# Cross attention: the first two tiles' scores placed among the last heads of the query phase

## The chip, the core and the metric

The kernel runs on one core of a Trainium2 chip. The metric is the device time of one execution in microseconds (us). Before the change it is 1665.28 us, the median of 3 runs (1662.88 to 1666.53). Abbreviations: PE is TensorE (PEld its weight loads), DVE is VectorE, ACT is ScalarE, POOL is GpSimd, SP is SyncE. SBUF is the working memory, PSUM the memory of 8 banks that PE writes to.

## What is computed

The reference is a decoder of four layers on `x` (8 sequences of 56 tokens, 256 channels). Each layer has self attention, cross attention to a context (8 sequences of 1500 positions, 64 channels) and a feed-forward part, each followed by a residual sum and a layer norm. The change touches three of the four cross attentions, those of layers 0, 2 and 3, which are built alike (16 heads of 128 channels, keys compressed to 64 channels; rotary queries in layers 0 and 2). For one sequence they compute

```
q      = x @ Wq                      # per head, 128 channels
qa     = rope(q @ w_kc_q) @ (W_qr @ W_kr.T)   # per head, 64 channels: the query against the compressed keys
e      = exp(scores - row maximum)   # scores = qa @ kv.T, 1500 positions
heads  = (e @ kv) / sum(e)
x      = layernorm(x + heads @ (w_kc_kv, Wo folded into one matrix wm))
```

Layer 3 has no rope, so its matrices are folded into one per head before `x` is touched.

## The kernel before

`decoder_kernel` runs twelve steps in order; a step's weights are loaded during the step before it by SP's DMA queue. The cross attention is `xattn` (line 686). It has two phases.

**Query phase** (pools `xq`, PSUM as two buffers of two banks and three of one bank, line 698). `x_weights` or `x_weights3` builds the small matrices, `turn_x` transposes X, and `x_context` starts the loads of the first two sequences' keys (`kvT`, on POOL's queue). Then `x_queries` (line 799, stages 1 and 2, which are layers 0 and 2) goes over the heads with a software pipeline: in round h it projects head h+3 (PE, one bank `ps_qh`; ACT copies it to `qh`), makes head h+2's rope (PE `ps_big`, two DVE multiplications, two POOL additions), and in odd rounds computes `qa` for the pair h-1, h with `pair_of` (line 744): 8 matmuls into one bank `ps_qk`, two ACT copies (line 754). Each half of `qa`'s 128 partitions holds one head of the pair; after every second pair two DMAs on ACT's queue (line 759) bring the columns of the last two pairs to the other half of the partitions. In rounds 3, 7 and 11 `rows_of` issues four DMAs on ACT's queue for a third of the first sequence's key rows (`kv`). `x_queries3` (line 761, stage 3, which is layer 3) has only `pair_of`, with `rows_of` ahead of heads 4, 8 and 12.

**Tile loop** (`x_tiles`, line 864; pools `xs` and `psx`, which take the memory of the query phase's, all 8 PSUM banks as one tile `ps_x`). A sequence has 16 x 56 = 896 queries, that is 7 tiles of 128; 8 sequences make 56 tiles. A tile n has two halves u; each covers 375 keys from the beginning and 375 from the middle of the 1500.

- `scored(n, u)` (891): the scores of a half, one matmul per half of the partitions (4 instructions in the trace), into two banks. There are four score banks, so two halves can be in flight.
- `moved(n, u)` (902): one DVE instruction copies the half to SBUF (`sc`, three buffers) and keeps its extremum in `tops`.
- `weights(n)` (917): ACT's exponential over the 1500 scores, with the sum.
- `turned(n)` (925): DVE's 32 x 32 block transpose into `cells` (the tile `eT`).
- `gather(b, j)` (932): PE's product of the transposed weights of sequence b with its `kv`, worked on during the tiles of sequence b+1.
- `weighted` and `kept` (947, 958): four portions of `wm`, made by PE and copied by ACT in rounds 0, 1, 13 and 20.

What sets the order: `ordered` (372, called `do` or, for matmuls, `pe` here) ties each instruction to the one that the program laid out before it on the same engine. All of `x_tiles` and `pair_of`'s matmuls are laid out so, and the query phase's other matmuls are held in program order too; ACT's copies, the ropes on DVE and POOL are not tied, the framework places them. Each engine then works its list in order. In the loop, round n lays out scores of half 1 of tile n+2 and half 0 of tile n+3, `moved(n+2, 0)`, what there is of `gather` and `weighted`, `turned(n)`, `moved(n+2, 1)` and `weights(n+1)`.

Of the kernel before, what the change touches and what calls it, by code (L numbers as in the profile page):

```python
# [9 lines left out]
F32 = mybir.dt.float32  # L10
# [15 lines left out]
KL = KB * NKB  # L26
# [238 lines left out]
class Decoder:  # L265
# [420 lines left out]
    def xattn(self, n):  # L686
        nc, tc = self.nc, self.tc
        qrT, krT = self.rowsets(f"l{n}x_r", 192), self.rowsets(f"l{n}x_k", DC)
        kckv, wo = self.rowsets(f"l{n}x_v", DC), self.rowsets(f"l{n}x_o", D)

        with tc.tile_pool(name="xa", bufs=1) as outer:


            wm = outer.tile([128, 8, D], F32, name="wm")


            qa = outer.tile([128, NB * NQ], F32, name="qa")
            with tc.tile_pool(name="xq", bufs=2) as pool, self.psum(2, 3):
                rotary = n != 3
                wqk = (self.x_weights if rotary else self.x_weights3)(pool, qrT, krT)  # L700
                self.turn_x(range(NT))
                context = self.x_context(outer)
                (self.x_queries if rotary else self.x_queries3)(n, pool, wqk, qa, context[2])
            with tc.tile_pool(name="xs", bufs=1) as pool, tc.tile_pool(name="psx", bufs=1, space=PSUM) as banks:
                self.x_tiles(pool, banks.tile([128, 8, 512], F32, name="ps_x"), qa, wm, kckv, wo, *context)

    def x_weights(self, pool, qrT, krT):

# [49 lines left out]
                rows, others = (slice(u * DC, (u + 1) * DC) for u in (odd, 1 - odd))  # L758
                nc.scalar.dma_start(flat[others, :, odd, cols], flat[rows, :, odd, cols])

    def x_queries3(self, n, pool, wqk, qa, rows_of):


        xT = self.xT
        kcq = [a.rearrange("p (j k) -> p j k", j=8) for a in self.parts(f"l{n}x_c")]
        wq = [a.rearrange("p (j k m) -> p j k m", j=2, k=2) for a in self.parts(f"l{n}x_q")]
        halves = [slice(odd * DC, (odd + 1) * DC) for odd in range(2)]

        m2 = pool.tile([128, 2, 8, DC], F32, bufs=1, name="m2")
        for four in range(2):  # L770
            ps = self.bank2("ps_m2")[:, :, : 4 * DC].rearrange("p u (j d) -> p u j d", d=DC)
            for j in range(4 * four, 4 * four + 4):
                for part in range(3):
                    for odd, rows in enumerate(halves):
                        self.ordered(
                            self.nc.tensor.matmul, ps[:, odd, j % 4], kcq[part][rows, j, :], wqk[rows, part, j],
                            start=part == 0, stop=part == 2,
                        )
            for k in range(2):
                self.by_parity(lambda rows, odd: (m2[rows, k, 4 * four : 4 * four + 4], ps[halves[k], odd]))  # L780
        m3 = pool.tile([128, 2, 8, 2, DC], F32, bufs=1, name="m3")
        for four in range(2):
            ps = self.bank2("ps_m3").rearrange("p u (j c d) -> p u j c d", c=2, d=DC)
            for j in range(4 * four, 4 * four + 4):
                for c in range(2):
                    for k in range(2):
                        for odd, rows in enumerate(halves):
                            self.ordered(
                                self.nc.tensor.matmul, ps[:, odd, j % 4, c],
                                wq[j // 2][rows, j % 2, k, c * 128 : (c + 1) * 128], m2[rows, k, j],  # L790
                                start=k == 0, stop=k == 1,
                            )
            self.by_parity(lambda rows, odd: (m3[:, odd, 4 * four : 4 * four + 4], ps[:, odd]))
        for h in range(0, 16, 2):
            if h and h % 4 == 0:
                rows_of(0, h // 4 - 1)
            self.pair_of(self.bank("ps_qk"), qa, h, [[(m3[:, odd, h // 2, c], xT[:, c, :]) for c in range(2)] for odd in range(2)])

    def x_queries(self, n, pool, wqk, qa, rows_of):
        xT, nc = self.xT, self.nc  # L800
        wq, kcq = self.heads(f"l{n}x_q"), self.rowsets(f"l{n}x_c", 192)

        def table(name):
            return self.const(name).rearrange("p (a s) -> p a s", a=2).unsqueeze(2).to_broadcast([96, 2, NB, S])

        cos, sin = table("xq_cos"), table("xq_sin")

        heads, ropes = {}, {}

        def projected(h):  # L810
            ps = self.bank("ps_qh")
            self.mm(ps[:, :T], [(wq(c, h), xT[:, c, :]) for c in range(2)], fixed=True)
            qh = heads[h] = pool.tile([128, T], F32, name="qh")
            nc.scalar.copy(qh, ps[:, :T])

        def rotated(h):
            qh = heads.pop(h)
            big = self.bank2("ps_big")
            for half in range(2):
                self.mm(big[:96, half, :T], [(kcq(h)[:, half * 96 : (half + 1) * 96], qh)], fixed=True)  # L820
            view = big[:96, :, :T].rearrange("p a (b s) -> p a b s", b=NB)
            rope = ropes[h] = pool.tile([96, 2, T], F32, bufs=5, name="rope")
            turn = pool.tile([96, 2, T], F32, name="turn")
            nc.vector.tensor_tensor(rope.rearrange("p a (b s) -> p a b s", b=NB), view, cos, ALU.mult)  # L824
            nc.vector.tensor_tensor(turn.rearrange("p a (b s) -> p a b s", b=NB), view, sin, ALU.mult)  # L825
            for half in range(2):
                nc.gpsimd.tensor_tensor(rope[:, half, :], rope[:, half, :], turn[:, 1 - half, :], ALU.add)  # L827


        for h in range(-3, 16):  # L830
            if h + 3 < 16:
                projected(h + 3)
            if 0 <= h + 2 < 16:
                rotated(h + 2)
            if h >= 0 and h % 2:
                if h % 4 == 3 and h < 12:
                    rows_of(0, h // 4)
                self.pair_of(
                    self.bank("ps_qk"), qa, h - 1,
                    [[(wqk(half, g), ropes[g][:, half, :]) for half in range(2)] for g in (h - 1, h)],  # L840
                )

    def x_context(self, pool):

        nc, kvs, kvTs = self.nc, {}, {}
# [15 lines left out]
        columns(1)  # L861
        return kvs, kvTs, rows_of, columns

    def x_tiles(self, pool, P, qa, wm, kckv, wo, kvs, kvTs, rows_of, columns):

# [8 lines left out]
        nc = self.nc  # L876
# [1 line left out]
        NI, NJ, CELL, do = 7, 6, 8 * KB, self.ordered  # L878
        mv = self.moments()
        sums, es, diags = {}, {}, {}  # L880
        sc4, acc = P[:, 0:4], P[:, 4:8]
        cells = pool.tile([128, NI * NI * CELL], F32, name="eT").rearrange("p (r c n) -> p r c n", r=NI, c=NI)
        scs = [pool.tile([128, KL], F32, name=f"sc{j}") for j in range(3)]
        for sc in scs:
            do(nc.gpsimd.memset, sc[:, L:], 0.0)
        num, other, rec = (pool.tile([128, 512], F32, name=name) for name in ("num", "other", "rec"))

        def pe(*args, **kw):
            do(nc.tensor.matmul, *args, **kw)

        def scored(n, u):
            b, i = divmod(n, NI)
            at = b * NQ + i * 128
            for half in range(2):
                rows = slice(half * DC, (half + 1) * DC)
                first = half * (HL - KB * (NKB - KP)) + u * QL
                pe(
                    sc4[:, 2 * u + half, :QL], qa[rows, at : at + 128], kvTs[b][rows, first : first + QL],
                    start=True, stop=True,
                )  # L900

        def moved(n, u):

            b, i = divmod(n, NI)
            if u == 0:
                if i == 0:
                    sums[b] = pool.tile([128, 8], F32, bufs=3, name="sums")
                es[n] = scs[n % 3], pool.tile([128, 4], F32, bufs=4, name="tops")
            sc, tops = es[n]
            halves = sc[:, :L].rearrange("p (u n) -> p u n", u=2)  # L910

            do(
                nc.vector.tensor_scalar, halves[:, :, u * QL : (u + 1) * QL], sc4[:, 2 * u : 2 * u + 2, :QL], 1.0,
                tops[:, 0:1] if u else None, ALU.mult, ALU.min, accum_out=tops[:, u : u + 1],
            )

        def weights(n):
# [3 lines left out]
                nc.scalar.activation,  # L921
                e[:, :L], e[:, :L], AF.Exp, bias=tops[:, 1:2], scale=-1.0, accum_out=sums[b][:, i : i + 1],
            )

        def turned(n):
            b, i = divmod(n, NI)
# [110 lines left out]
            do(nc.vector.bn_aggr, mv[:, t, :], st)  # L1037

        end, wms = NB * NI, (0, 1, 13, 20)
        for n in range(2):  # L1040
            for u in range(2):
                scored(n, u)
                moved(n, u)
        weights(0)
        scored(2, 0)
        for n in range(end):
            b, i = divmod(n, NI)
# [16 lines left out]
                    output(t, 1)  # L1064
            elif n in wms:
                weighted(wms.index(n))
            turned(n)
            if n + 2 < end:
                moved(n + 2, 1)
            if n + 1 < end:  # L1070
                weights(n + 1)
            if n in wms:
                kept(wms.index(n))
# [825 lines left out]
```

## Time and profile before

| | |
|---|---|
| median of 3 runs | 1665.28 us |
| the profiled execution's own time | 1665.35 us |
| its span | 1663.1 us (37875 instructions) |
| busy share of the span | PE 90%, DVE 66%, ACT 38%, POOL 19% |
| mean granted clock of PE | 0.926 |
| score matmuls `ps_x<-kvT,qa` | x1344, 310.4 us busy |
| block transposes `eT<-sc` | x168, 297.1 us busy, mean 1768 ns |
| reduces `sc<-ps_x`, first and second half | x168 each, means 936 and 959 ns |
| exponentials `sc<-sc,tops` | x168, mean 1544 ns |

The 168 are 56 tiles in three stages. The stages by the trace, from the first score matmul to the end of the tile loop and its tail: 219.3 to 451, 851.4 to 1085 and 1355.9 to 1590 us. A row of busy times counts an instruction from start to end, so neighbours on DVE that overlap a little show more than their spacing. A wait is named by what ended last before it; where that had long been done, it was something else. The granted clock is the share of PE's full clock that its throttle let through.

### The profile page before, as it was taken

The page shows a single profiled execution, that of the slowest core. Times are in us where ns is not written, and L with a number is a line of the kernel's source. Part 1 is how long each engine was busy: PE and PEld are TensorE (multiplying, and loading weights), DVE is VectorE, ACT ScalarE, POOL GpSimd, SP SyncE. Part 2 cuts the span into 40 slices and gives each one's busy share as a digit, 9 for nine tenths or more (in the row PEclk, how much of TensorE's full clock was granted, in tenths as well). Part 3 has the DMA queues.
Part 4 walks back from the last instruction along what each step waited for, and adds up shares of the span by engine and source line. Part 5 has one row for each costly group of instructions (what it writes and reads, how often), then busy time and mean ns, then how long its engine had stood idle before and what let it go on. Part 6 is the DMA issues. An engine that isn't in the chain of part 4 may idle for free.

```text
span 1663.1 us, 37875 instructions
## 1 busy us (share of the span) xinstructions
PE 1499.5 (90%) x16428; PEld 894.4 (54%) x16428; DVE 1095.2 (66%) x1793; ACT 625.2 (38%) x915; POOL 323.9 (19%) x302
## 2 busy tenths in 40 slices
PE   7989989999788678998989999899987978999898
PEld 4666435556644344565435555655555834555656
DVE  0575579999475855326569999635474239999633
ACT  2431245655312422103245556332343144566320
POOL 4711511212123010011521122101131000221200
PEclk9999979999897878999988999999997987999989
DMA  9523422323020001222332322121220361323100
GB/s 359 188 79 108 123 56 84 96 83 88 18 87 28 26 27 35 78 70 74 114 86 62 110 78 81 41 64 55 83 64 27 119 172 38 104 72 88 41 1 11
DMA packets 52088, 133.76 MB, mean 80 GB/s; under 512 B 20673, under 2 KB 21137, under 8 KB 51922
## 3 DMA queue, kind: packets, MB, share of 16 engines
q1 hardware_dynamic: 19906, 65.36, 12.0%
q10 hardware_dynamic: 28368, 50.25, 10.8%
q0 software_dynamic: 3648, 15.73, 2.9%
q8 instruction: 129, 2.11, 0.5%
q14 instruction: 37, 0.30, 0.1%
HBM read 119.06 MB, written 6.75 MB: 76 GB/s over the span
## 4 chain that ended last, share of the span: by engine, by line
PE 49%; DVE 9%; issue 8%; ACT 2%; DMA 1%; POOL 1%; ACTq 1%; DVEq 0%; POOLq 0%
PE ps_x L376 17%; PE ps_glu L368 8%; PE ps_y L368 7%; PE ps_qk L1675 2%; DVE sc L376 2%; PE ps_v L1675 2%; PE ps_qh L368 2%; PE ps_big L368 1%; PE ps_y L1675 1%; PE ps_q L368 1%; PE ps_qk L376 1%; PE ps_m L376 1%; PE ps_s L1397 1%; DVE E L1418 1%; DVE mx L1415 1%
## 5 line engine op out<-in xcount | busy, mean ns | idle before, releaser
L376 PE MATMUL ps_x<-kvT,qa 64*128 64x375 f32 x1344 | 310.4, 567 | 29.1 <-DVE sc L376 23.1
L376 ACT ACTIVATE sc<-sc,tops 128x1500 f32<-128x1500 f32 x168 | 259.2, 1544 | 151.7 <-DVE sc L376 118.3
L376 DVE STREAM_TRANSPOSE eT<-sc 128x1536 f32<-128x1536 f32 x168 | 297.1, 1768 | 11.7 <-PE ps_x L376 9.5
L376 PE MATMUL ps_x<-eT,kv 32*64 32x224 f32 x9024 | 257.7, 357 | 3.7 <-issue 3.2
L376 PEld LDWEIGHTS ps_x<-eT,kv 32*64 32x64 f32 x9024 | 197.6, 133 | 70.1 <-issue 59.8
L376 PEld LDWEIGHTS ps_x<-kvT,qa 64*128 64x128 f32 x1344 | 114.3, 201 | 187.2 <-DVE sc L376 160.4
L376 DVE TENSOR_SCALAR_CACHE_REDUCE sc<-ps_x 128x750 f32<-128x750 f32 x168 | 157.3, 936 | 38.4 <-PE ps_x L376 38.2
L376 DVE TENSOR_SCALAR_CACHE_REDUCE sc<-ps_x,tops 128x750 f32<-128x750 f32 x168 | 161.1, 959 | 1.3 <-PE ps_x L376 1.1
L376 POOL TENSOR_TENSOR eT<-eyes,sums 128x224 f32<-128x224 f32 x24 | 13.3, 555 | 453.6 <-DVE sums L376 453.6
L827 POOL TENSOR_TENSOR rope<-rope,turn 96x448 f32<-96x448 f32 x64 | 71.0, 1130 | 65.0 <-DVE turn L825 65.0
L824 DVE TENSOR_TENSOR rope<-ps_big,consts 96x896 f32<-96x896 f32 x32 | 34.8, 1086 | 58.4 <-PE ps_big L368 58.4
L1190 ACT ACTIVATE act<-ps_glu 128x448 f32<-128x448 f32 (+1 forms) x52 | 28.3, 544 | 111.7 <-PE ps_glu L368 108.4
L1194 DVE TENSOR_TENSOR act<-ps_glu,act 128x448 f32<-128x448 f32 x43 | 26.8, 624 | 65.2 <-ACT act L1190 65.1
L418 ACT ACTIVATE rstd<-rstd 112x3 f32<-112x3 f32 (+2 forms) x21 | 4.3, 204 | 166.2 <-DVE rstd L417 166.1
L624 DVE RECIPROCAL rec<-rec 128x896 f32<-128x896 f32 x8 | 46.0, 5753 | 27.0 <-ACT rec L623 27.0
L376 PE MATMUL ps_x<-wm,qa 128*112 128x128 f32 (+1 forms) x336 | 53.5, 318 | 9.7 <-DVE qa L376 9.7
L450 DVE TENSOR_TENSOR X<-X,ps_y 112x256 f32<-112x256 f32 x32 | 13.5, 421 | 70.6 <-PE ps_y L368 70.6
L376 PEld LDWEIGHTS ps_x<-wm,qa 128*112 128x112 f32 x336 | 45.2, 191 | 21.7 <-issue 11.2
L1758 POOL TENSOR_TENSOR qk<-qk,sw 128x896 f32<-128x896 f32 x16 | 33.3, 2083 | 101.3 <-DVE sw L1757 78.8
L376 POOL TENSOR_TENSOR qa<-num,rec 64x448 f32<-64x448 f32 x42 | 47.9, 1140 | 2.9
L754 ACT COPY qa<-ps_qk 64x448 f32<-64x448 f32 x48 | 25.3, 527 | 60.0 <-PE ps_qk L376 46.1
L376 POOL DMA_DIRECT2D kvT<-kvT x24 | 13.7, 573 | 122.7 <-DVE X L450 49.2
(410 smaller groups left out, 2424.2 us busy)
## 6 DMA issues: line engine op xcount, KB each, us to landing
kv<-kv ACTq DMA_DIRECT2D x288, 128.0 KB, 2.7
kvT<-kvT POOLq DMA_DIRECT2D x24, 384.0 KB, 3.5
qa<-qa ACTq DMA_DIRECT2D x24, 224.0 KB, 3.6
raw<-in_ctx ACTq DMA_DIRECT2D x6, 512.0 KB, 4.3
kv<-raw POOLq DMA_DIRECT2D x6, 512.0 KB, 4.2
kvT<-by POOLq DMA_DIRECT2D x6, 512.0 KB, 4.3
l0a_q<-in_l0a_q SPq DMA_DIRECT2D x4, 512.0 KB, 10.6
l0a_c<-in_l0a_c SPq DMA_DIRECT2D x4, 512.0 KB, 8.8
```

What stands on the lines that cost most here:

```text
L368: ins = self.nc.tensor.matmul(out, lhsT, rhs, start=n == 0, stop=n == len(terms) - 1)
L376: call(*args, **kw)
L624: nc.vector.reciprocal(rec, rec)
L754: nc.scalar.copy(flat[rows, :, odd, h // 2 * S : (h // 2 + 1) * S], ps[rows, :T].rearrange("p (b s) -> p b s", b=NB))
L824: nc.vector.tensor_tensor(rope.rearrange("p a (b s) -> p a b s", b=NB), view, cos, ALU.mult)
L827: nc.gpsimd.tensor_tensor(rope[:, half, :], rope[:, half, :], turn[:, 1 - half, :], ALU.add)
L1190: nc.scalar.activation(act, ps[:m, 0, :T], AF.Silu)
L1194: nc.vector.tensor_tensor(act, ps[:m, 1, :T], act, ALU.mult)
L1397: tc.keep_in_program_order(nc.tensor.matmul(*args, **kw))
L1415: nc.vector.tensor_reduce(mx, view, AX.X, ALU.max)
L1675: tc.keep_in_program_order(nc.tensor.matmul(*args, **kw))
L1758: nc.gpsimd.tensor_tensor(qk, qk, sw, ALU.add)
```

## The change

The generator `x_tiles` is now started before the query phase ends. `scored`, `moved` and `weights` of tiles 0 and 1 are laid out in four portions inside the query phase: in `x_queries` after rounds 9, 10, 13 and 14 (each portion a half of a tile, with the exponential behind the second half), in `x_queries3` after heads 8 and 10 (one portion each) and 14 (two). For this a two-bank PSUM tile of its own, `ps_x`, holds one half at a time; it comes out of the query phase's PSUM, which keeps two one-bank buffers in place of three. `sc`, `sums` and `tops` move to the pool that lasts through both phases. Once the tile loop's memory is there, the loop begins with the transposes of tiles 0 and 1 together and the scores of tile 2. Rounds 0 and 1 then have no transpose of their own, and their exponentials are those of tiles 2 and 3; round 2 has none.

```diff
-            with tc.tile_pool(name="xq", bufs=2) as pool, self.psum(2, 3):
+            with tc.tile_pool(name="xq", bufs=2) as pool, self.psum(2, 2):
...
+                tiles = self.x_tiles(outer, qa, wm, kckv, wo, *context)
+                tiles.send(None)
+                tiles.send(self.psa.tile([128, 2, 512], F32, name="ps_x"))
+                (self.x_queries if rotary else self.x_queries3)(n, pool, wqk, qa, context[2], tiles)
...
+                try:
+                    tiles.send((pool, banks.tile([128, 8, 512], F32, name="ps_x")))
+                except StopIteration:
+                    pass
...
+            for _ in range({8: 1, 10: 1, 14: 2}.get(h, 0)):
+                next(tiles)
...
+            if h in (9, 10, 13, 14):
+                next(tiles)
...
+        first = yield
+        sc_of = lambda u: first
+        scs = [outer.tile([128, KL], F32, name=f"sc{j}") for j in range(3)]
...
+        for n in range(2):
+            for u in range(2):
+                yield
+                scored(n, u)
+                moved(n, u)
+            weights(n)
+        pool, P = yield
+        sc4, acc = P[:, 0:4], P[:, 4:8]
+        sc_of = lambda u: sc4[:, 2 * u : 2 * u + 2]
...
-        for n in range(2):
-            for u in range(2):
-                scored(n, u)
-                moved(n, u)
-        weights(0)
+        turned(0)
+        turned(1)
         scored(2, 0)
...
-            turned(n)
+            if n > 1:
+                turned(n)
             if n + 2 < end:
                 moved(n + 2, 1)
-            if n + 1 < end:
+
+            if n < 2:
+                weights(n + 2)
+            elif 2 < n + 1 < end and n != 2:
                 weights(n + 1)
```

More of the change, by code (lines that the diff above doesn't have):

```diff
@@ L702, in xattn @@
                 context = self.x_context(outer)
-                (self.x_queries if rotary else self.x_queries3)(n, pool, wqk, qa, context[2])
+                tiles = self.x_tiles(outer, qa, wm, kckv, wo, *context)
+                tiles.send(None)
+                tiles.send(self.psa.tile([128, 2, 512], F32, name="ps_x"))
+                (self.x_queries if rotary else self.x_queries3)(n, pool, wqk, qa, context[2], tiles)
             with tc.tile_pool(name="xs", bufs=1) as pool, tc.tile_pool(name="psx", bufs=1, space=PSUM) as banks:
-                self.x_tiles(pool, banks.tile([128, 8, 512], F32, name="ps_x"), qa, wm, kckv, wo, *context)
+                try:
+                    tiles.send((pool, banks.tile([128, 8, 512], F32, name="ps_x")))
+                except StopIteration:
+                    pass
     def x_weights(self, pool, qrT, krT):
@@ L759, in pair_of, with x_queries3 @@
                 nc.scalar.dma_start(flat[others, :, odd, cols], flat[rows, :, odd, cols])
-    def x_queries3(self, n, pool, wqk, qa, rows_of):
+    def x_queries3(self, n, pool, wqk, qa, rows_of, tiles):
         xT = self.xT
@@ L797, in x_queries3, with x_queries @@
             self.pair_of(self.bank("ps_qk"), qa, h, [[(m3[:, odd, h // 2, c], xT[:, c, :]) for c in range(2)] for odd in range(2)])
-    def x_queries(self, n, pool, wqk, qa, rows_of):
+            for _ in range({8: 1, 10: 1, 14: 2}.get(h, 0)):
+                next(tiles)
+    def x_queries(self, n, pool, wqk, qa, rows_of, tiles):
         xT, nc = self.xT, self.nc
@@ L862, in x_context, with x_tiles @@
         return kvs, kvTs, rows_of, columns
-    def x_tiles(self, pool, P, qa, wm, kckv, wo, kvs, kvTs, rows_of, columns):
+    def x_tiles(self, outer, qa, wm, kckv, wo, kvs, kvTs, rows_of, columns):
         nc = self.nc
@@ L880, in x_tiles @@
         sums, es, diags = {}, {}, {}
-        sc4, acc = P[:, 0:4], P[:, 4:8]
-        cells = pool.tile([128, NI * NI * CELL], F32, name="eT").rearrange("p (r c n) -> p r c n", r=NI, c=NI)
-        scs = [pool.tile([128, KL], F32, name=f"sc{j}") for j in range(3)]
+        first = yield
+        sc_of = lambda u: first
+        scs = [outer.tile([128, KL], F32, name=f"sc{j}") for j in range(3)]
         for sc in scs:
             do(nc.gpsimd.memset, sc[:, L:], 0.0)
-        num, other, rec = (pool.tile([128, 512], F32, name=name) for name in ("num", "other", "rec"))
         def pe(*args, **kw):
@@ L897, in scored @@
                 pe(
-                    sc4[:, 2 * u + half, :QL], qa[rows, at : at + 128], kvTs[b][rows, first : first + QL],
+                    sc_of(u)[:, half, :QL], qa[rows, at : at + 128], kvTs[b][rows, first : first + QL],
                     start=True, stop=True,
@@ L906, in moved @@
                 if i == 0:
-                    sums[b] = pool.tile([128, 8], F32, bufs=3, name="sums")
-                es[n] = scs[n % 3], pool.tile([128, 4], F32, bufs=4, name="tops")
+                    sums[b] = outer.tile([128, 8], F32, bufs=3, name="sums")
+                es[n] = scs[n % 3], outer.tile([128, 4], F32, bufs=4, name="tops")
             sc, tops = es[n]
@@ L912, in moved @@
             do(
-                nc.vector.tensor_scalar, halves[:, :, u * QL : (u + 1) * QL], sc4[:, 2 * u : 2 * u + 2, :QL], 1.0,
+                nc.vector.tensor_scalar, halves[:, :, u * QL : (u + 1) * QL], sc_of(u)[:, :, :QL], 1.0,
                 tops[:, 0:1] if u else None, ALU.mult, ALU.min, accum_out=tops[:, u : u + 1],
@@ L923, in weights @@
             )
+        for n in range(2):
[7 more added lines that the diff above has]
+        sc_of = lambda u: sc4[:, 2 * u : 2 * u + 2]
+        cells = pool.tile([128, NI * NI * CELL], F32, name="eT").rearrange("p (r c n) -> p r c n", r=NI, c=NI)
+        num, other, rec = (pool.tile([128, 512], F32, name=name) for name in ("num", "other", "rec"))
         def turned(n):
```

## The prediction

> **What bounds the kernel now.** I read the page's 40 slices first, then the busy times in stretches of 10 us through the three cross attentions, then the instructions in order of time where each tile loop begins. The slices show PE high throughout, and DVE full in three blocks of some 230 us: the tile loops of the three cross attentions.
>
> ```profile
> PE   7989989999788678998989999899987978999898
> DVE  0575579999475855326569999635474239999633
> PEclk9999979999897878999988999999997987999989
> ```
>
> That first line looks as if PE were the bound everywhere. The stretches tell it apart (columns: length, busy time with instructions of PE, PEld, DVE, ACT, POOL, then granted clock, DMA share, GB/s): 200 to 210 is the query phase, 210 to 220 its tail, the others tile loop.
>
> ```profile
> 200.00:210.00 10.00, 10.00 (x31) 4.20 (x30) 4.56 (x5) 2.65 (x5) 5.77 (x6) 1.00 0.31 83
> 210.00:220.00 10.00, 7.33 (x21) 1.94 (x21) 3.69 (x4) 2.11 (x4) 4.57 (x7) 0.78 0.22 70
> 230.00:240.00 10.00, 7.34 (x40) 3.12 (x40) 10.00 (x14) 5.37 (x7) 0.00 (x0) 0.80 0.30 87
> 320.00:330.00 10.00, 9.83 (x176) 6.37 (x174) 10.00 (x17) 6.90 (x12) 3.76 (x5) 1.00 0.19 54
> ```
>
> The query phase is bound by PE (10.00 of 10), the tile loop by DVE (10.00), at 3.44 us a tile: two reduces of 0.86 to 0.89 and a transpose of 1.69, start to start. So what the change does is to move four reduces from where DVE is the bound to where it is half idle, and their matmuls from where PE has gaps to where it is the bound. What counts is when DVE's full stretch begins. Stage 1:
>
> ```profile
> 212.61 1.08 DVE L825 TENSOR_TENSOR turn<-ps_big,consts 96x896 f32<-96x896 f32 x1
> ...
> 218.20 1.08 ACT L754 COPY qa<-ps_qk 64x448 f32<-64x448 f32 x2 [4.34 <-PE ps_qk L376]
> ...
> 218.76 1.29 ACTq L759 DMA_DIRECT2D qa<-qa  x2
> 219.33 0.50 PEld L376 LDWEIGHTS ps_x<-kvT,qa 64*128 64x128 f32 x4 [2.63 <-ACT qa L754]
> ...
> 221.22 0.94 DVE L376 TENSOR_SCALAR_CACHE_REDUCE sc<-ps_x 128x750 f32<-128x750 f32 x1 [7.54 <-PE ps_x L376]
> ...
> 226.29 0.94 DVE L376 TENSOR_SCALAR_CACHE_REDUCE sc<-ps_x 128x750 f32<-128x750 f32 x1
> ...
> 229.88 1.76 PE L376 MATMUL ps_x<-kvT,qa 64*128 64x375 f32 x8 [0.61 <-DVE sc L376]
> ...
> 236.76 2.87 PE L376 MATMUL ps_x<-kvT,qa 64*128 64x375 f32 x8 [1.68 <-DVE sc L376]
> ```
>
> Tile 0's first reduce is at 221.22, tile 2's at 226.29, tile 4's at 233.18 (6.89 later, with two transposes between). From tile 4 on, both kernels do the same on DVE, so **tile 4's first reduce is my marker**: 233.18, 865.05 and 1369.74 in the three stages. Eight score matmuls (two halves) take 1.76 at full clock and 2.87 at the lower one: 0.88 or 1.44 a half.
>
> **A wait that is hidden now.** Tile n of a batch takes columns 128n to 128n+127 of the queries, 56 to a head pair: tiles 0 and 1 need pairs 0 to 4, tile 2 needs pairs 4 to 6, and pair 6 is exchanged between the partition halves by the last DMAs, issued at 218.76. These land after
>
> ```profile
> DMA to landing us min/median/max: 3.3/3.6/5.5
> ```
>
> so at 222.2. Before, tiles 0 and 1 are worked on meanwhile. After, nothing but two transposes is left to cover it, and tile 2 is the first on PE.
>
> **The sum, stage 1.** (a) PE: two of the four moved halves stand before the last rope's matmuls in PE's order: 2 x 0.88 = 1.76. PE has no gap there (10.00), so this counts in full: the last DVE `turn` ends at 213.69 + 1.76 = 215.45. (b) Behind it on DVE is tile 1's first reduce, 1.0, to 216.5; the second half of tile 1 has the same PSUM tile and waits for it, 0.9, to 217.4; its reduce 0.2 + 1.0, to 218.6; the exponential 1.54 + 0.1, to 220.3. The last head pair's matmuls, behind that half on PE (217.4 + 1.72 for a pair, and 0.3 until seen), are done by 219.4. (c) The copies of that pair come after the exponential in ACT's order: first copy 0.53, to 220.9. (d) DMA: 3.4 (this stage's faster one), to 224.3. (e) Tile 2's first half after an idle PE: 1.8 (219.33 to 221.22 was 1.89, the same in stage 3 1.80), so its reduce is at 226.1, against 226.29 now. The two transposes (3.4, from 219.5) lie under this wait. (f) From there to the marker DVE has four reduces with no transpose between and waits for PE: slot free 1.0, three halves, the `weighted` block of 16 matmuls (1.15 now), 0.3 to the reduce. At full clock 1.0 + 2.64 + 1.15 + 0.3 = 5.1; at the lower one, all times 2.87/1.76, 1.0 + 4.3 + 1.9 + 0.3 = 7.5. I take the middle, 6.3, since the stretches of the loop's start show both clocks. Marker: 232.4. **Gain 0.8** (2.0 to -0.4).
>
> **Stage 2** has the same queue: last `turn` ends at 846.69 + 1.76 = 848.45, the same 10.65 to the reduce of tile 2, 859.1, and 6.3: 865.4 against 865.05. **-0.35** (0.85 to -1.55). It was the better one before, as PE kept its clock in the tail (copies at 850.30).
>
> **Stage 3** has no ropes and is held by ACT's own queue:
>
> ```profile
> 1351.24 2.40 ACTq L376 DMA_DIRECT2D kv<-kv  x4
> ...
> 1353.68 2.17 ACT L754 COPY qa<-ps_qk 64x448 f32<-64x448 f32 x4 [3.25 <-issue]
> 1355.33 1.29 ACTq L759 DMA_DIRECT2D qa<-qa  x2
> ```
>
> The copies start when the issue of the key rows ends (1351.24 + 2.40). Tile 0's first half, behind head 8 on PE, waits for the exchange issued at 1343.87 (3.4 to 4.1): 1347.3 to 1348.0, and holds head 10, then a pair at the lower clock (3.08 for the last one now): to about 1351.5. Copies, then the second half's reduce, to 1353.5; the table load (1.28) and the exponential; behind them the key rows' issue (2.40), to 1357.2; heads 12 and 14 to 1358.8 (first copy of 14); DMA 3.4 to 4.7 (4.7 in this stage's last); 1.8: tile 2's reduce at 1364.0 to 1365.3, and 6.3: 1370.9 against 1369.74. **-1.2** (0.65 to -3.1).
>
> Together -0.75: I forecast no measurable change, **1665.35 (the profiled execution's own time, span 1663.1) + 0.75 = 1666.1 us**, with the terms' ends 1661.9 to 1670.4. The median of the runs, 1665.28, is 0.07 from it.
>
> Costed at nothing: the third one-bank PSUM buffer taken away (a head pair's bank is free 1.25 after its matmuls, and asked for again 2.7 after, now with two; without that cover every pair stalls PE); reduces on DVE in the query phase (4.56 of 10 busy); memsets on POOL (0.17), moved ahead of the ropes; the table load, moved. A wait goes at the loop's start (tile 0's score), and the exchange DMA is late next.
>
> **Two rules weighed.** The trace: from 240 to 250, where PE works in bursts, the granted clock is 0.50. The Trainium skill (TensorE: Matmul & The Clock Gate, Part 1) says that an idle window of some 3.4 us halves the clock and about as much sustained work restores it; it speaks against this change, which opens a hole of 219.4 to 224.3. An estimate by that page: 3.4 us at half clock cost 1.7, 6.8 in place of 6.3, in sum 1667.6.
> The trace: ACT stood still behind its own DMA issue up to 1353.68. The same page (Architectural detail) calls ACT strictly first in, first out; where it is not, the copies of (c) pass the exponential and the sum is 1663.5.
>
> **Rivals.** *Faster, a: copies first, clock up.* If the program's order puts the last copies ahead of tile 1's exponential, (c) shrinks by 1.2 (219.1 for 220.3) and by 1.4 in stage 2; if PE also keeps its clock, 3 x 1.2 more: 1666.1 - 2.6 - 3.6 = 1659.9. For it: nothing but the order in which the program is laid out ties the two. Against: the exponential is ready first by these rows. *Faster, b: DVE alone counts.* All of 221.22 to 226.29 goes, and 4.84 and 5.15 in the others: 15.1, 1650.3. Against: the DMA above.
> *Slower.* The first exponential (tile 0: table load 1.28 + 1.64) lies among ACT's copies of projected heads. If it stands ahead of a copy that is ready before it, that copy is done some 3 to 4 us late, the two one-bank buffers are both taken, and PE, the bound here, waits. Counted from the end of head 12's rope matmuls, PE does the half to 0.9, head 14 to 2.4, head 13's rope to 3.9, pair 10 to 5.5, and then wants head 14's bank for head 15. ACT meanwhile: ropes on DVE to 2.8, reduce to 3.9, load and exponential to 6.8, only then head 14's copy, to 7.4. That is 1.9 in each of two stages: 1666.1 + 3.8 = 1669.9. It decides from 1.5 us of delay on, which is the slack of the bank; with the lower clock too, 1673.5. *It does not do what it says*: the halves wait for their exchange and run in the tail; then four reduces are only moved by a few us, and the time stays within the forecast's range.
>
> **Numbers.** A measurement of this kernel tells about 0.2% from no change, 1662.0 to 1668.6. Forecast 0.36 and "does not do" 0.04, so the same 0.40; faster 0.24 (a 0.18, b 0.06); slower 0.36. The range leaves out b and the far ends: 1658.5 to 1672.5.
>
> **What would show it.** Query phase: 1.76 us longer up to the last `turn`. ACT: exponential, then the last copies. PE: a hole of 4 to 5 us before tile 2, ended by a DMA. DVE: two transposes back to back inside that hole, then reduces that wait for PE. From the first projected head's copy in stage 1 (153.40) to the marker: 79.8 now, 79.0 forecast. I am wrong if tile 2's scores start without the hole, if heads in the middle of the query phase are further apart than 7.87 us a pair plus 1.8, or if DVE is not full behind the marker.

## The result, and the profile after

The changed kernel takes 1659.52 us, the median of 20 runs (1650.76 to 1664.83), beside 1661.63 us for 20 runs of the kernel before (1652.88 to 1666.53). The ratio is 0.999, with a 95% interval of 0.9976 to 1.0005: no change that can be told. The profiled execution took 1663.11 us, with a span of 1661.3. Ratios here and below are those of fast runs; one execution of a control kernel, at 4867 us, is not among them.

The page's slices for the changed kernel: DVE's three blocks stand as they did, and the clock nearly so.

```profile
DVE  1574579999476765326569999635464239999632
PEclk9999979999898878999988999999997988999989
```

The span is 1.8 us shorter than before, but not by the change. Stage 1 begins (first `ps_wqk` matmul) at 144.46 in place of 146.73, so 2.27 were gone before the first changed instruction. From a stage's beginning, before against after, to the points named in the prediction:

| us from the stage's beginning | stage 1 | stage 2 | stage 3 |
|---|---|---|---|
| last group of copies in the query phase | 71.47, 73.42 | 71.04, 73.89 | 37.47, 40.11 |
| third tile's first reduce | 79.56, 79.15 | 78.90, 79.54 | 46.64, 48.47 |
| marker: fifth tile's first reduce | 86.45, 86.42 | 85.79, 86.29 | 53.53, 54.73 |
| last transpose of the loop | 272.01, 271.93 | 273.19, 273.38 | 237.76, 237.80 |

By the marker the three stages gained 0.03 and lost 0.50 and 1.20 us; by the loop's end even that is level. Four reduces a stage have left the full stretch of DVE, and nothing came of it. Stage 1 of the changed kernel in order of time shows where it went (start, us, engine, what, and in brackets the idle time before with what ended it):

```profile
212.20 1.08 DVE L834 TENSOR_TENSOR turn<-ps_big,consts 96x896 f32<-96x896 f32 x1
...
215.06 1.80 PE L376 MATMUL ps_qk<-rope,wqk 96*64 96x448 f32 x8
...
216.22 1.54 ACT L376 ACTIVATE sc<-sc,tops 128x1500 f32<-128x1500 f32 x1 [2.76 <-DVE sc L376]
216.97 3.44 DVE L376 STREAM_TRANSPOSE eT<-sc 128x1536 f32<-128x1536 f32 x2 [0.78 <-PE ps_qk L376]
...
217.88 1.08 ACT L760 COPY qa<-ps_qk 64x448 f32<-64x448 f32 x2
...
219.01 0.89 PE L376 MATMUL ps_x<-kvT,qa 64*128 64x375 f32 x2 [2.15 <-ACT qa L760]
...
221.87 4.37 PE L376 MATMUL ps_x<-kvT,qa 64*128 64x375 f32 x10 [1.97 <-DMA qa<-qa]
...
223.61 0.94 DVE L376 TENSOR_SCALAR_CACHE_REDUCE sc<-ps_x 128x750 f32<-128x750 f32 x1 [3.21 <-PE ps_x L376]
...
226.17 2.03 PE L376 MATMUL ps_x<-l0x_o,l0x_v 128*64 128x128 f32 x16
...
229.80 1.00 DVE L376 TENSOR_SCALAR_CACHE_REDUCE sc<-ps_x,tops 128x750 f32<-128x750 f32 x1 [2.56 <-PE ps_x L376]
...
230.88 0.94 DVE L376 TENSOR_SCALAR_CACHE_REDUCE sc<-ps_x 128x750 f32<-128x750 f32 x1
```

The last `turn` starts 67.74 after the stage's beginning, 65.88 before: the two halves on PE ahead of it. The pair's copies start at 217.88, when the exponential is done, not at about 217.0, when their matmuls are. PE then does the matmul whose queries were copied directly (219.01) and stands until the exchange DMA brings the others (221.87). DVE, done with its two transposes at 220.4, waits 3.21 us. And then it waits again, 2.56 us at 229.80, because the `weighted` block of 16 matmuls lies between the halves on PE. The stretches of 4 us say at what clock that was (columns as in the prediction):

```profile
216.00:220.00 4.00, 1.75 (x8) 0.37 (x4) 3.22 (x4) 2.69 (x4) 0.00 (x0) 1.00 0.06 12
220.00:224.00 4.00, 2.13 (x6) 1.17 (x6) 0.79 (x2) 0.00 (x0) 0.00 (x0) 0.54 0.54 105
224.00:228.00 4.00, 4.00 (x22) 2.13 (x20) 2.52 (x6) 1.64 (x2) 0.00 (x0) 0.50 0.00 0
```

PE falls to half clock in the hole and does the loop's first matmuls there, busy for all of 224 to 228. The half clock as such is not new. The kernel before had it at the same place, ahead of the loop and in its first tiles:

```profile
216.00:220.00 4.00, 2.83 (x6) 0.91 (x6) 0.00 (x0) 1.05 (x2) 0.40 (x4) 0.50 0.00 0
220.00:224.00 4.00, 3.97 (x14) 1.81 (x12) 2.03 (x5) 0.62 (x1) 0.00 (x0) 0.50 0.59 115
```

### The profile page after: what moved, and what is told of

Same layout as the page of the kernel before. It is cut to its first block, busy times and chain, and to the rows that moved or that the text cites. A ratio compares the mean times of both kernels' runs of the same rounds, so it can differ in the third digit from the quotient of the medians.

```text
span 1661.3 us, 37855 instructions
## 1 busy us (share of the span) xinstructions
PE 1492.6 (90%) x16428; PEld 893.5 (54%) x16428; DVE 1094.7 (66%) x1793; ACT 624.6 (38%) x915; POOL 323.6 (19%) x302
## 3 DMA queue, kind: packets, MB, share of 16 engines
q10 hardware_dynamic: 28368, 50.25, 10.7%
HBM read 119.06 MB, written 6.75 MB: 76 GB/s over the span
## 4 chain that ended last, share of the span: by engine, by line
PE 49%; DVE 10%; issue 7%; ACT 2%; DMA 1%; ACTq 0%; POOL 0%; DVEq 0%
PE ps_x L376 17%; PE ps_glu L368 8%; PE ps_y L368 7%; PE ps_qk L1700 3%; DVE sc L376 2%; PE ps_v L1700 2%; PE ps_qh L368 2%; PE ps_big L368 1%; PE ps_y L1700 1%; PE ps_q L368 1%; PE ps_qk L376 1%; DMA qa<-qa 1%; PE ps_m L376 1%; PE ps_s L1422 1%; DVE E L1443 1%
## 5 line engine op out<-in xcount | busy, mean ns | idle before, releaser
L823 ACT COPY qh<-ps_qh 128x448 f32<-128x448 f32 x32 | 17.0, 532 | 57.3 <-PE ps_qh L368 57.3
```

## The experiments

The theory (A in the expectations): what DVE saves is given back in four places, namely PE's halves in the query phase, the copies behind the exponential, the exchange DMA that nothing covers any more, and PE's order at the loop's start. The rivals are B, that PE's own work and clock bound the start and the DMA is only what ends last; C, that the lost PSUM buffer eats the gain; D and E, in the expectations where they are tested. The markers come from one profile a run. For the kernel before and its two controls they agree within 0.1 us in stages 1 and 2, but in stage 3 they lie between 51.67 and 53.53, so stage 3 tells less. A time under about 0.2% is not told from none.

### Copies ahead of the exponential

```diff
+            if n == 1:
+                yield
             weights(n)
...
-            if h in (9, 10, 13, 14):
+            if h in (9, 10, 13, 14, 15):
```

(and 14: 3 in place of 14: 2 in stage 3, where the order stays as it was.)

> The exponential of tile 1 is laid out behind the last head pair's copies and DMAs instead of ahead of them. Marker: from a stage's first ps_wqk matmul to the first reduce of the fifth tile; in the changed kernel 86.42, 86.29 and 54.73 us, in the kernel before 86.45, 85.79 and 53.53. Theory A (the gain is held up by the chain last pair's copies, exchange DMA, tile 2's scores): in stage 1 the pair is done at 216.9 and copied from 217.88, so the copies, the DMA and tile 2's reduce come 0.9 us earlier, marker 85.5 and 85.4; stage 3 has this order already, 54.7. In sum 1.8 us, 0.1% of the time. Theory B (the start is bound by PE's matmuls or by the transposes, the DMA only happens to end last): markers unchanged within 0.3.

Measured: last copies at 72.44 and 72.90, 0.98 and 0.99 earlier, third tile's reduce 78.04 and 78.17, 1.1 and 1.4 earlier; markers 84.38, 85.29 and 53.65. The chain of A holds in both stages, with stage 1's marker a further 0.9 lower (the eight score matmuls behind the first `weighted` block took 1.53 in place of 2.70, so PE had its full clock back sooner). Stage 3, where nothing was altered, came out 1.1 lower too. Ratio to before 0.998 (0.9957 to 1.0004): the time alone doesn't tell it. In stage 1 of this run the copies are ahead of the exponential, and the DMA still ends PE's wait:

```profile
218.69 1.08 ACT L760 COPY qa<-ps_qk 64x448 f32<-64x448 f32 x2 [3.44 <-PE ps_qk L376]
...
220.58 1.54 ACT L376 ACTIVATE sc<-sc,tops 128x1500 f32<-128x1500 f32 x1 [0.82 <-DVE eT L376]
...
222.64 4.28 PE L376 MATMUL ps_x<-kvT,qa 64*128 64x375 f32 x10 [1.93 <-DMA qa<-qa]
```

### The third tile doesn't need the exchange

```diff
+        def tile_of(n):
+            b, i = divmod(n, NI)
+            return b, i if b else (0, 1, 4, 5, 2, 3, 6)[i]
...
-            b, i = divmod(n, NI)
+            b, i = tile_of(n)
```

(in `scored`, `weights` and `turned`.)

> The changed kernel, with the first sequence's tiles taken in the order 0, 1, 4, 5, 2, 3, 6. Tiles 4 and 5 need head pairs 1 to 5 only, so the third tile no longer reads what the last exchange DMA brings. Theory A (that DMA is the new wait): PE's second half-matmul no longer waits from 219.0 to 221.87; the third tile's reduce follows the two transposes (end 220.4 in the changed kernel's stage 1) in place of 223.61, 2.8 us earlier in stages 1 and 2, and nothing in stage 3, where the transposes end at 1362.9 and the reduce follows at 1362.94. Markers about 83.6, 83.5 and 54.7, or a little lower if PE keeps its clock; the time 5 to 7 us under the changed kernel, ratio to before about 0.995. Theory B (PE's own work and its clock bound the start): the wait is taken over by PE, markers within 0.5 of 86.4, 86.3 and 54.7, ratio 0.999.

Measured: third tile's reduce at 75.87, 76.78 and 46.88, that is 3.3, 2.8 and 1.6 earlier; markers 82.98, 83.20 and 53.87. Ratio to before 0.9939 (0.9918 to 0.9961). In stage 1 of this run the reduce follows the transposes without a wait:

```profile
218.92 3.44 DVE L376 STREAM_TRANSPOSE eT<-sc 128x1536 f32<-128x1536 f32 x2 [0.78 <-PE ps_qk L376]
219.84 1.08 ACT L760 COPY qa<-ps_qk 64x448 f32<-64x448 f32 x2
...
220.97 1.88 PE L376 MATMUL ps_x<-kvT,qa 64*128 64x375 f32 x8 [2.15 <-ACT qa L760]
222.28 0.90 DVE L376 TENSOR_SCALAR_CACHE_REDUCE sc<-ps_x 128x750 f32<-128x750 f32 x1
```

The line at 220.97 is all four instructions of a half and the next half's, where the changed kernel did two and waited for the DMA. So the wait is real, and B falls for the first part of the start. In stage 3, where none was expected, 1.6 of the third tile's reduce came; in the changed kernel the third tile waited there for the transposes, and these for tile 1's two halves (below). The first of these waited for an exchange DMA until 1354.90 and the second took 1.57 at half clock; in this run each took 0.90, without that wait. The edit doesn't touch tile 1, so this 1.6 is not put down to it.

### The same order in the kernel before

The same edit on the kernel before.

> The kernel before, with the first sequence's tiles in the order 0, 1, 4, 5, 2, 3, 6, as a control for the same edit on the changed kernel. Theory A: the exchange DMA was hidden before behind tiles 0 and 1 (issued at 218.76, landed 222.2, the third tile's scores only due at 224.9), so nothing moves: markers 86.45 and 85.79, in stage 3 between 51.7 and 53.5 (it has differed by that much between executions), ratio 1.000. Theory D (the order of tiles is worth something by itself): markers down by 2 to 3 us here too, ratio 0.995.

Measured: markers 86.43, 85.79 and 53.35; ratio 1.0001 (0.998 to 1.0021). The order is worth nothing that can be told there: the exchange was hidden, and the change has laid it bare. D falls.

### Two one-bank buffers alone

`self.psum(2, 3)` becomes `self.psum(2, 2)` in the kernel before.

> The kernel before, with two one-bank PSUM buffers in the query phase in place of three, and nothing else changed. Theory A (a bank is free 1.25 us after a pair and wanted 2.7 after): markers as before, 86.45, 85.79 and 53.53, within 0.3; the time unchanged. Theory C (the lost buffer costs the gain): the query phase is longer, some 0.3 us a pair, markers 2 to 3 us up in stages 1 and 2; time 4 to 6 us up.

Measured: markers 86.47, 85.78 and 51.67; ratio 1.0005 (0.9985 to 1.0025). Stages 1 and 2 are as before, and stage 3's lower marker goes with the clock (under "Not settled"). The buffer alone costs nothing; C falls. In the changed kernel, where PE also has the halves to do, 0.2 us at most is left for it: the last `turn` came 1.86 later, and the two halves ahead of it on PE take 0.83 each from their start to the next matmul's.

### `wm` made three rounds later

```diff
-        end, wms = NB * NI, (0, 1, 13, 20)
+        end, wms = NB * NI, (3, 4, 13, 20)
```

> The changed kernel, with the first two portions of the matrix wm made in rounds 3 and 4 in place of 0 and 1. From the third tile's reduce to the fifth's the changed kernel takes 7.27, 6.75 and 6.26 us, in which DVE has work for 3.6 only. Theory A (f: PE's order holds it, two blocks of 16 matmuls stand between the halves, 1.15 to 2.0 us each, though the second is not ahead of the fifth tile's first half): one block less, 1.2 to 2.0 us, so 5.3, 5.0 and 4.8, and markers 1.5 lower each; in sum 4 us, ratio to before 0.997. Theory B (the score matmuls at the lower clock alone hold it): markers within 0.5 of 86.4, 86.3 and 54.7.

Measured: from the third tile's reduce to the fifth's 4.67, 5.34 and 4.92, where the changed kernel had 7.27, 6.75 and 6.26; markers 83.83, 84.87 and 53.29; ratio to before 0.9966 (0.9944 to 0.9989). In stage 1 of this run the reduces come one after another from 228.24 on:

```profile
228.24 0.94 DVE L376 TENSOR_SCALAR_CACHE_REDUCE sc<-ps_x 128x750 f32<-128x750 f32 x1 [0.51 <-PE ps_x L376]
229.31 1.00 DVE L376 TENSOR_SCALAR_CACHE_REDUCE sc<-ps_x,tops 128x750 f32<-128x750 f32 x1
230.24 0.93 DVE L376 TENSOR_SCALAR_CACHE_REDUCE sc<-ps_x 128x750 f32<-128x750 f32 x1
```

This is (f) of the prediction, and B, which had the markers within 0.5 of the changed kernel's, falls for this part too. Before the change these blocks cost DVE nothing, since a transpose stood beside them and no wait came behind. From the kernel before, stage 1:

```profile
227.16 1.77 DVE L376 STREAM_TRANSPOSE eT<-sc 128x1536 f32<-128x1536 f32 x1
...
228.13 1.15 PE L376 MATMUL ps_x<-l0x_o,l0x_v 128*64 128x128 f32 x16
...
228.86 0.96 DVE L376 TENSOR_SCALAR_CACHE_REDUCE sc<-ps_x,tops 128x750 f32<-128x750 f32 x1
```

### Only tile 0 in the query phase

```diff
-        for n in range(2):
+        for n in range(1):
             for u in range(2):
                 yield
...
-        turned(0)
-        turned(1)
+        for u in range(2):
+            scored(1, u)
+            moved(1, u)
```

(portions after rounds 9 and 10 alone, the loop as in the kernel before.)

> The changed kernel with only tile 0 worked on in the query phase; tile 1 stays at the loop's start, and no two transposes stand together. Theory A: the queries are as late as in the changed kernel (two halves ahead of the last ropes on PE), but tile 1's reduces cover the DMA and the transposes lie between the reduces as before. Last copies 1.3 to 1.7 us later than before, third tile's reduce 5.7 after them in place of 8.0, then 6.89: markers 85.4 and 85.3, stage 3 about 53; ratio to before 0.999, in the traces 1 us a stage under the changed kernel. If half the moved reduces bring half of the saving that DVE alone would have (theory E, DVE's work decides): markers 84.0 and 83.4.

Measured: markers 85.00, 86.30 and 53.13; ratio to before 0.9995 (0.998 to 1.001). From the last copies to the third tile's reduce 5.60 in stages 1 and 2, as expected, and then 6.89. In stage 2 the copies came 2.77 later than before, not 1.7, hence 1.0 over the expectation: 1.85 is the last `turn`, and the last pair's six matmuls took 2.97 where the kernel before took 2.06. E falls: it had 2.4 less in each of stages 1 and 2, and they came out 1.45 lower and 0.5 higher. Half of the moved reduces bring no half of DVE's saving.

### Tile 0 alone, in the gap at the end of the query phase

As the last one, with the portions after rounds 13 and 14 in stages 1 and 2: `if h in (13, 14)`.

> As with one tile alone, but its two halves are laid out in rounds 13 and 14 of stages 1 and 2, behind the last ropes' matmuls, where PE waits for POOL; stage 3 is as with one tile alone. Theory A: the 1.76 us that the two halves cost in the full part of the query phase are gone, the last copies come at most 0.5 us later than before, and the exponential and its table load stand ahead of them on ACT (up to 1.3 more): markers 84.0 to 85.5 and 83.5 to 85, some 0.5 to 1.5 under one tile in rounds 9 and 10. If PE's query phase has slack after all, both are the same.

Measured: last `turn` at 65.89 and 66.35, as before the change, where tile 0 in rounds 9 and 10 had it at 67.75 and 68.21; last copies at 71.56 and 72.03, 0.09 and 0.99 later than before (0.5 at most was expected); markers 83.54, 84.49 and 53.02; ratio to before 0.9957 (0.9931 to 0.9984). The lines of stage 1:

```profile
211.36 0.90 PE L376 MATMUL ps_x<-kvT,qa 64*128 64x375 f32 x4
...
213.34 0.90 PE L376 MATMUL ps_x<-kvT,qa 64*128 64x375 f32 x4 [1.07 <-DVE sc L376]
214.17 1.80 PE L376 MATMUL ps_qk<-rope,wqk 96*64 96x448 f32 x8
```

The halves lie where PE waited for POOL, and the last pair takes 1.80 for its 8 matmuls, where the kernel before took 2.97 for six of them. So the 1.8 us of PE in the full part of the query phase was a real price. By the markers of stages 1 and 2, one tile in the right place beats two in the wrong one; by the time the two intervals still overlap.

### Both the order and `wm` later

> The changed kernel with both: the first sequence's tiles in the order 0, 1, 4, 5, 2, 3, 6, and the first two portions of wm made in rounds 3 and 4. If the wait for the exchange and PE's share at the loop's start are two separate terms, they add up: third tile's reduce as with the tile order alone (75.9, 76.8 and 46.9 after the stage's start), and from there to the fifth's 4.7, 5.3 and 4.9 as with wm later alone: markers 80.6, 82.1 and 51.8, ratio to before 0.990 to 0.993. If they are one and the same wait: markers as with the tile order alone, 83.0, 83.2 and 53.9, ratio 0.994.

Measured: markers 81.20, 81.80 and 52.03; ratio to before 0.9931 (0.9915 to 0.9948), median 1647.76. The two terms add up, within 0.6 us a stage: from the kernel with the changed order alone to this one the markers fall by 1.8, 1.4 and 1.8. The time by itself doesn't tell the two apart. This run beats both kernels (before, beside it, 1659.18): its markers lie 5.3, 4.0 and 1.5 under those of the kernel before, 10.7 of the 15.1 us that the prediction's rival "DVE alone counts" had priced. So in stages 1 and 2 most of the saving on DVE was there, once the DMA and PE's order were out of its way. In its stage 1 PE goes on without a hole from 221.56:

```profile
220.59 0.90 DVE L376 TENSOR_SCALAR_CACHE_REDUCE sc<-ps_x 128x750 f32<-128x750 f32 x1
221.56 6.44 PE L376 MATMUL ps_x<-kvT,qa 64*128 64x375 f32 x20 [0.57 <-DVE sc L376]
...
225.93 0.94 DVE L376 TENSOR_SCALAR_CACHE_REDUCE sc<-ps_x 128x750 f32<-128x750 f32 x1 [0.44 <-PE ps_x L376]
```

## Why the prediction was right, step by step

- **The number.** The forecast of 1666.1 is 6.6 over the measured 1659.52. Of this 3.7 is the level that it was counted from: one execution of 1665.35, where 20 runs of the kernel before have a median of 1661.63. The rest is +0.75 forecast beside a difference of -2.1 in the medians, and neither can be told from none. What the prediction got right is that nothing measurable would come, and why in stages 1 and 2.
- **(a) PE in the query phase.** Forecast 1.76, measured 1.86 in stage 1 (the last `turn`). Shown by tile 0 in the gap: there the `turn` came as early as before the change, and the copies 0.95 and 1.78 earlier than with tile 0 in rounds 9 and 10.
- **(b) to (e), from the end of that `turn` to the third tile's reduce.** Forecast 10.65, measured 10.33 (213.28 to 223.61). Both waits in it are shown: the copies behind the exponential by the first experiment, the DMA by the order of tiles. The cover that was missing was named rightly: the control on the kernel before found nothing to gain.
- **(f) the loop's start.** Forecast 6.3 between 5.1 and 7.5; measured 7.27, 6.75 and 6.26. Stage 1's missing gain (0.8 forecast, 0.03 measured) is this term, mis-sized by 1.0: PE came to it at half clock and stayed there longer than the middle that I took. The `weighted` block alone took 2.03 in place of 1.15.
- **Stage 2:** forecast -0.35, measured -0.50. **Stage 3:** forecast -1.2, measured -1.20, but by another road than the prediction's, so this agreement is chance. There the DMA was not last (issued at 1356.22, landed 3.4 later); PE was at the third tile's scores from 1359.61 on, under the transposes:

```profile
1352.55 1.54 ACT L376 ACTIVATE sc<-sc,tops 128x1500 f32<-128x1500 f32 x1
...
1354.58 2.16 ACT L760 COPY qa<-ps_qk 64x448 f32<-64x448 f32 x4 [0.39 <-PE ps_x L376]
...
1358.45 1.00 DVE L376 TENSOR_SCALAR_CACHE_REDUCE sc<-ps_x,tops 128x750 f32<-128x750 f32 x1 [1.67 <-PE ps_x L376]
1359.38 3.64 DVE L376 STREAM_TRANSPOSE eT<-sc 128x1536 f32<-128x1536 f32 x2
...
1362.94 0.90 DVE L376 TENSOR_SCALAR_CACHE_REDUCE sc<-ps_x 128x750 f32<-128x750 f32 x1
```

  Tile 1's two halves are both laid out behind head 14 and share one PSUM tile; the second one's reduce ends at 1359.4, the transposes come behind it on DVE, and the third tile follows at once. The prediction's queue for stage 3 has no term for these two halves. The step that failed is "heads 12 and 14 to 1358.8 (first copy of 14); DMA 3.4 to 4.7": the key rows' issue went on beside the exponential, the copies started 40.11 after the stage's beginning where the prediction had 41.0, and the transposes that it put under the DMA were what ended last.
- **Costed at nothing:** the lost PSUM buffer cost nothing that shows, as said. The rival with the exponential ahead of a projected head's copy did not come about: in stage 1 head 14's copy (202.89) stands before the table load (203.44).
- **The two rules weighed.** In stage 1 the granted clock was 1.00 in 216 to 220, 0.54 in 220 to 224 and 0.50 in 224 to 228. PE's hole of 216.86 to 221.87 had 0.89 of work in it and no idle stretch above 2.15, and the clock stayed at 0.50 through 8.6 us without a gap (221.87 to 230.5). The Trainium skill (TensorE: Matmul & The Clock Gate, Part 1), which spoke against the change, has the direction right: a hole, then half clock. Its times, some 3.4 us idle and about as much work to come back, are not those measured, and the measurement decides. So it is luck in part that the 6.8 estimated from it for (f) was nearer to the measured mean of 6.76 than my 6.3: it counts 3.4 us at half clock, less than half of stage 1's 8.6. The copies waited for the exponential, and were 1.0 earlier when it was laid out behind them, which agrees with what the same page (Architectural detail) says of ACT's order.

Not settled: whether the changed kernel is truly 0.1% faster, and what sets PE's clock where stage 3's loop begins. That clock goes with the 1.9 us by which stage 3's marker differs between like kernels. The last copies start at 37.45 to 37.47 after the stage's beginning in the kernel before and both controls, but from 40 to 46 us the granted clock was 0.50 and 0.51 in the two with markers of 53.53 and 53.35, and 1.00 in the one with 51.67. That PE's clock is the reason for stage 1's extra 1.0 in (f) was read from the stretches, not tried by itself.

## What to carry to other kernels

To move work off the bounding engine helps only as far as the next thing can start earlier: follow the chain to the first instruction that both kernels have in common, and ask of each transfer what covers it once its neighbours are gone. A tile order that needs late data last cost nothing that can be told and gave about 3 us in two of three stages here. Move work into the gap of the engine that has to do it, not just into a phase in which the relieved engine is idle.

## What the runs showed that was not expected

- A half's two matmuls wait one by one: the one with its own rows ran at 219.01, the other at 221.87, when the DMA had landed.
- DMA issues on ACT's queue go on while an exponential that the program lays out before them runs: key rows issued from 1351.67 to 1354.54, the exponential from 1352.55 to 1354.09.
- With PE's gap at the end of the query phase filled, its clock stayed up in stage 1: 1.00 at the last pair (1.80 for 8 matmuls), against 0.50 before (2.97 for six). In stage 2 the kernel before kept 1.00 there without it (2.06 for six), so the filling is not shown to be the only cause.
